# Four graph layers on 32 graphs: new orders on ScalarE and GpSimd at the start, an earlier transposed adjacency matrix, and another order inside layer 1

## The chip, the cores and the metric

The kernel runs on one core of one Trainium2 chip. A core has TensorE (PE, matmuls, with its weight loads listed as PEld), VectorE (DVE), ScalarE (ACT), GpSimd (POOL) and SyncE (SP), whose queue issues all DMAs of this kernel. The metric is the device time of one execution in microseconds. A profile shows one execution; its span runs from the first instruction to the last.

## The reference

`x` holds 32 graphs of 512 nodes with 128 features, `adj` one 512 x 512 matrix for all of them. Four layers follow each other, each adding to x what it makes of `h = max(layernorm(x), 0)`:

```python
# layer 0: attention weights from adj's pattern alone, diagonal and rest with weights of their own
idx = jnp.cumsum(m.reshape(-1).astype(jnp.int32)) - 1          # m = adj > 0
A = jax.nn.softmax(jnp.where(m, e[0][idx].reshape(adj.shape), NEG), axis=1)
out = einsum('ij,bjg->big', A * M, h @ W[0]) + einsum('ij,bjg->big', A * (1 - M), h @ W[1]) + bias
# layer 1: xs = [h, h A, 2 h A A - h, h A, 2 h A A - h] with A = adj (nodes are the contracted axis)
out = jax.nn.relu(concat(xs) @ Theta1 + bias)
# layer 2: weights = adj * adj
messages = jnp.einsum('nm,bnd->bmd', weights, relu(h @ psi_w + psi_b))
out = relu(concat(messages, h) @ phi1_w + phi1_b) @ phi2_w + phi2_b
# layer 3: attention masked by adj
A = jnp.exp(8 * jnp.tanh(Q K^T / sqrt(128) / 8)) * adj;  out = (A / A.sum(-1)) @ h @ v
```

## The kernel before, in words

**Tiles.** Two graphs make a quad, 16 in all; two quads (A and C) make a round, eight rounds, for layers 0 and 1. Layers 2 and 3 go quad by quad. All matmuls that matter are float32.

**Products.** A 512 x 512 matrix times the features of a round is split into 2 x 2 blocks and made with seven block products instead of eight (`products`, L359, in the order `ORDER`, with PSUM banks a, c and d). Their right operands are differences of blocks (`right_steps`, L341, tiles rt_g, rt_h, rt_w, rt_feat, one 128x512 subtraction each, on the engines listed in `engs`); product 6 needs the second of them, and the second is made from the first. Each product's result is taken from its bank by `evict`, mostly on VectorE.

**Beginning (L165 to L680).** By an order written out by hand (`manual_schedule`: all instructions of PE, DVE, ACT and POOL stand as the source has them) the attention matrix of layer 0 is made while the first quads are normalised. Statistics of quads 0 and 1 (`early_stats`) go over POOL, which raises to a power (L211) and multiplies (L212); ScalarE then makes h from x, eight 128x128 tiles a quad (L241). PE turns h (p_hT), ScalarE copies it to hT (L262), and PE projects it (p_g, L428). POOL also makes three parts of e (L556 to L567), which VectorE uses at L607 in `at_part`; `score_rows` (L622, L626) and `softmax_rows` (L633 to L635) make the attention rows. `keep_busy(n)` (L493) issues n matmuls whose result is not used.

**Layer 0 (`round0`, L758).** Also in the order of the source. In the loop over the seven products other work is put in between by hand: `turn(q)` makes hT of quad q (two VectorE transposes into hb at L277, four SP DMAs to the DRAM tile d_hT at L284, one SP DMA back as hT at L286), `projection(q)` makes p_g from hT, `normalise(q)` makes h, `stats` the statistics. `squares` is `turn_adj` (L472): four VectorE transposes of adj (tile adj_squares, L477) and four SP DMAs of 256 KB to adjT_d (L481); layer 3 reads it much later. Before, it stands in round 1: three transposes at product index 1 (L873), the fourth and the DMAs at index 4 (L892). In round 1 p_g of quad 4 comes at index 1, that of quad 5 at index 5; in round 2 p_g of quad 6 comes at index 1.

**Layer 1 (`layer1`, L923).** From here a scheduler places the instructions; generators that take turns (L1133 on) set the order of the source. For a quad, `first` makes x1T = h adj (seven products, p_x1T, evicted by ScalarE and VectorE) and a copy hs; `weighed` projects hs and x1T to w (p_w, 32 matmuls in two banks, copied by ScalarE at L946); then the seven products of adj with w, to whose banks `own` adds projections of hs (p_l, L755). In before a round's steps are: first(A), then first(C) and weighed(A), then weighed(C) and right2 (rt_w, all on POOL), then the products, at the end of them bank e with the fourth own block. Rounds follow each other two steps apart, so PE's order is: products of r, first(C) of r+1, both weighed of r+1, first(A) of r+2, products of r+1.

**Layer 3 (`layer3`).** Scores (p_score), tanh and exponential on ScalarE (L1086, L1088), times adj's transpose (L1090, in turn on VectorE and POOL), then p_av (L1100).

Of the kernel before, what the change touches and what calls it, by code (L numbers as in the profile page):

```python
# [24 lines left out]
def kernel(  # L25
# [106 lines left out]
    def spread(w, n):  # L132
        return w[:, None, :].to_broadcast([P, n, D])

    for b in range(4):
        load_x(b)
    ecol = const.tile([P, NK], F32, name="ecol")
    nc.sync.dma_start(ecol, e_l0.rearrange("o (k p) -> p (o k)", p=P))
    elast = const.tile([P, 1], F32, name="elast")
    nc.sync.dma_start(elast, bass.AP(tensor=e_l0.tensor, offset=e_l0.offset + NE - 1, ap=[[0, P], [1, 1]]))  # L140
    qw = load_rows(q_w, "qw")[:, 0, :]
    kw = load_rows(k_w, "kw")[:, 0, :]
    w0 = const.tile([P, 2, D], F32, name="w0")
# [212 lines left out]

    ORDER0 = (ORDER[0], ORDER[4]) + ORDER[1:4] + ORDER[5:]

    def products(name, form, left, right, evict, order=ORDER):  # L359

        banks = {}
        for k, g, first in order:
            if first:
                banks[g] = bank(f"p_{name}_{g}")
            form(banks[g], left[k], right[k], first)
            evict(k, banks[g])
            yield

# [140 lines left out]
    for t in range(NT):  # L509
        for s in range(t + 1):  # L510
            nc.tensor.matmul(pi[:, t : t + 1], upto[:, s, blk(t)], rch[:, s : s + 1],
                             start=(s == 0), stop=(s == t))
    keep_busy(4)
    early = [early_stats(q, q == 1) for q in range(2)]
    next(early[0])

# [4 lines left out]
    before = prep.tile([P, NT], F32, name="before")  # L521
    nc.vector.tensor_sub(before, incl, rc)
    nc.vector.tensor_scalar(known[:, :, 0], before, float(NE), None, OP.min)
    h = {q: normed_tile(q) for q in range(3)}
    hT = {q: feature_major(f"hT0_{q}") for q in range(4)}
    normal = [normed_steps(q, h[q]) for q in range(3)]
# [24 lines left out]
    nc.scalar.copy(pgs[:, 0:2, :], pg[0])  # L551
    nc.vector.tensor_copy(pgs[:, 2:4, :], pg[1])
    nc.scalar.copy(qkT, tiles(p)[:, :2, :])

    elastn = prep.tile([P, 1], F32, name="elastn")
    nc.gpsimd.tensor_scalar(elastn, elast, -1.0, None, OP.mult)  # L556
    ecoln = prep.tile([P, NK], F32, name="ecoln")
    nc.gpsimd.tensor_scalar(ecoln, ecol, -1.0, None, OP.mult)

    parts = []  # L560
    for i in range(3):
        eh = prep.tile([P, NK], BF16, name=f"eh_{i}")
        nc.gpsimd.tensor_copy(eh, ecoln)
        part = prep.tile([P, NK], F32, name=f"part_{i}")
        nc.gpsimd.tensor_copy(part, eh)
        if i < 2:
            nc.gpsimd.tensor_sub(ecoln, ecoln, part)  # L567
        parts.append(part)
    row_of = prep.tile([P, NK], F32, name="row_of")
    nc.vector.tensor_copy(row_of, pb[:, :, 1])  # L570

# [33 lines left out]
    for kk in range(NK):  # L605
        for i in range(3):
            nc.vector.tensor_scalar(at_part[:, i, kk, :], cols, col_of[:, kk : kk + 1],  # L607
                                    parts[i][:, kk : kk + 1], OP.is_equal, OP.mult)
    go(normal[1], 3)
    go(turned[0])  # L610
    next(project[0])
    go(normal[1])
# [145 lines left out]
    def round0(r):  # L758
# [52 lines left out]
        for i, _ in enumerate(products(f"l0_{r}", by_token, sums["att"], now, evict,  # L811
                                          ORDER if r else ORDER0)):
            if r == 0:
                if i == 0:
                    transpose_rows(pt, att, 2)
                    transpose_rows(pt, att, 3)
                    att_copies((0, 1, nc.scalar.copy), (1, 1, nc.vector.tensor_copy))
                    next(left_of_att)
                    next(left_of_att)
                    go(early_stats_2)  # L820
                    att_copies((2, 1, nc.scalar.copy), (3, 1, nc.scalar.copy))
                elif i == 1:
                    for t in range(NT):
                        nc.tensor.matmul(p_adiag[:, blk(t)], ones, diag[:, t, :], start=True, stop=True)
                    nc.scalar.copy(adiag[0], p_adiag)
                    go(normal[2], NT + 1)
                    diagonal_of(0, 0)
                    go(ln3, NT + 1)
                    go(normal[2])
                    next(left_of_att)  # L830
                    next(left_of_att)
                    go(ln3)
                elif i == 2:
                    diagonal_of(0, 1)
                    add(1, 0, 0)
                elif i == 3:
                    next(turned[2])
                    go(turned[2])
                    add(0, 1, 1)
                    bias(0)  # L840
                    normalise(3)
                    go(ahead[4], NT)
                elif i == 4:
                    upper(held["a"])
                    turned.append(pe_steps(h[3], "hT0_3", hT[3]))
                    next(turned[3])
                    go(ahead[4])
                    add(1, 1, 2)
                    go(projection(2))
                    go(turned[3])  # L850
                    normalise(4)
                    go(ahead[5], NT)
                    bias(1)
                    go(turn(4))
                    go(ahead[5])
                elif i == 5:
                    go(projection(3))
                    go(right_of(1))
                    diagonal_of(1, 0)
                    normalise(5)  # L860
                elif i == 6:
                    go(stats_c, NT)
                continue
            if i == 0:
                if C + 2 < NQ:
                    go(turn(C + 2))
                if A + 4 < NQ:
                    normalise(A + 4)
                diagonal_of(r, 1)
                add(1, 0, 0)  # L870
            elif i == 1:
                add(0, 1, 1)
                if r == 1:  # L873
                    go(squares, 3)
                if more:
                    go(projection(A + 2))
                go(stats_a, NT + 1)
                go(own_a, NT)
                if more:
                    bias(r + 1)  # L880
                go(stats_a)
                go(own_a)
            elif i == 3:
                add(1, 1, 2)
                if not more:
                    next(next_layer)
                if C + 4 < NQ:
                    normalise(C + 4)
                if r >= 3:
                    go(sums_ahead, 2)  # L890
            elif i == 4:
                if r == 1:  # L892
                    go(squares, 3)
                if A + 4 < NQ:
                    go(turn(A + 4))
            elif i == 5:
                if more:
                    go(projection(C + 2))
                    go(right_of(r + 1))
                    diagonal_of(r + 1, 0)  # L900
                go(stats_c, NT + 1)
                go(own_c, NT)
            elif i == 6:
                go(stats_c)
# [18 lines left out]
    def layer1(r):  # L923
# [29 lines left out]
        first(A)  # L953
        turned(C)
        yield
        first(C)
        w1 = quad_tile(f"w_{r}").rearrange("p w e -> p (w e)")[:, : 4 * N]
        w1 = w1.rearrange("p (t b w f) -> p t b w f", t=NT, b=2, w=2)
        weighed(A)
        yield  # L960
        weighed(C)
        right2 = right_blocks(lambda J, b: w1[:, 2 * J : 2 * J + 2, b], f"w_{r}", [nc.gpsimd] * 4)
        yield
        u = [u_tile(f"l1_{r}_{i}") for i in range(3)]
        held = {}

# [2 lines left out]

        def each(y):  # L970
            return y.rearrange("p w (i f) -> p w i f", i=2)

        def spread_bias():
            return b1[:, None, None, :].to_broadcast([P, 2, 2, D])

        def finish(y, I, b):
            x = x_block(r, I, b).rearrange("p w i f -> p w (i f)")
# [6 lines left out]
        def evict(k, p):  # L984
            pv = of_pairs(halves(p))
            if k == 1:
                nc.vector.tensor_add(each(u[0]), pv, spread_bias())
            elif k == 6:
                nc.vector.tensor_add(each(u[1]), pv, each(u[0]))
            elif k == 5:  # L990
                held["d"] = pv
            elif k == 7:
                nc.vector.tensor_add(each(u[2]), pv, each(u[0]))
                nc.vector.tensor_add(each(u[2]), held["d"], each(u[2]))
            elif k == 2:
                own(p, 0, 0, False)
                y = work.tile([P, 2, H], F32, tag="rt", name=f"y1_{r}", bufs=6)
                nc.vector.tensor_add(each(y), pv, spread_bias())
                finish(y, 0, 0)
            elif k == 4:  # L1000
                own(p, 1, 0, False)
                done(p, u[0], 1, 0)
            elif k == 3:
                own(p, 0, 1, False)
                done(p, u[1], 0, 1)

        for _ in products(f"l1_{r}", by_token, sums["adj"], right2, evict):
            pass
        p = bank(f"p_l1_{r}_e")
        own(p, 1, 1, True)  # L1010
        done(p, u[2], 1, 1)
        yield
        if C == NQ - 1:
            yield
            yield
        ln_stats(A)
# [47 lines left out]
    def layer3(q):  # L1064
# [5 lines left out]
        for b in range(2):  # L1070
# [15 lines left out]
                nc.scalar.activation(ex[:, t, :], ps, AF.Tanh, scale=1.0 / (8.0 * math.sqrt(D)))  # L1086
            for t in range(NT):
                nc.scalar.activation(ex[:, t, :], ex[:, t, :], AF.Exp, scale=8.0)  # L1088
                eng = nc.gpsimd if t % 2 else nc.vector
                eng.tensor_mul(split(ex[:, t, :]), split(ex[:, t, :]), crossed(adjTx[0][:, t, :]))  # L1090
            yield
            out_r = out[2 * q + b].rearrange("(t p) f -> p t f", p=P)
# [86 lines left out]
```

## Time and profile before

| | |
|---|---|
| three timed runs | 981.59, 982.46, 981.39 us; median 981.59 |
| the profiled execution | 980.04 us, its span 977.9 us |
| granted TensorE clock, mean | 0.995 |
| matmuls, by stage | beginning to 35.5 us, layer 0 to 196.6, layer 1 to 489.7 (layer 2's first ones mixed in before that), layer 2 to about 692, layer 3 to the end |

A line of the time-ordered list gives the start and duration in microseconds, engine, source line, operation, what is written and read, sizes, and how many instructions were merged; in brackets stands how long the engine had been idle and what ended that. A line of the stage table gives a stretch of time, the busy microseconds and instructions of PE, PEld, DVE, ACT and POOL, then the granted TensorE clock, the busy share of the DMA engines and their GB/s. A line of the list of waits gives who waited for whom, in total, how often, and the longest.

### The profile page before, as it was taken

The page shows a single profiled execution, that of the slowest core. Times are in us where ns is not written, and L with a number is a line of the kernel's source. Part 1 is how long each engine was busy: PE and PEld are TensorE (multiplying, and loading weights), DVE is VectorE, ACT ScalarE, POOL GpSimd, SP SyncE. Part 2 cuts the span into 40 slices and gives each one's busy share as a digit, 9 for nine tenths or more (in the row PEclk, how much of TensorE's full clock was granted, in tenths as well). Part 3 has the DMA queues.
Part 4 walks back from the last instruction along what each step waited for, and adds up shares of the span by engine and source line. Part 5 has one row for each costly group of instructions (what it writes and reads, how often), then busy time and mean ns, then how long its engine had stood idle before and what let it go on. Part 6 is the DMA issues. An engine that isn't in the chain of part 4 may idle for free.

```text
span 977.9 us, 15160 instructions
## 1 busy us (share of the span) xinstructions
PE 959.3 (98%) x5470; PEld 782.7 (80%) x5470; DVE 578.5 (59%) x1322; ACT 471.5 (48%) x1055; POOL 430.1 (44%) x473
## 2 busy tenths in 40 slices
PE   7998999999999999999999999999999999999998
PEld 4788999988988988989977777777667776777776
DVE  6776887656356446557568666556654544444444
ACT  4773453442332232376728544545574455444553
POOL 4676798844437532430624433344132332223322
PEclk8999999999999999999999999999999999999999
DMA  9046554162231311444333333322132121121111
GB/s 256 9 130 173 151 151 114 43 169 65 95 121 44 87 44 44 109 106 110 87 108 99 98 86 85 87 79 73 55 86 77 44 76 54 54 76 44 54 33 44
DMA packets 83914, 86.04 MB, mean 88 GB/s; under 512 B 6785, under 2 KB 74625, under 8 KB 83841
## 3 DMA queue, kind: packets, MB, share of 16 engines
q1 hardware_dynamic: 83840, 85.09, 30.9%
q8 instruction: 43, 0.70, 0.3%
q14 instruction: 31, 0.25, 0.1%
HBM read 44.17 MB, written 40.89 MB: 87 GB/s over the span
## 4 chain that ended last, share of the span: by engine, by line
PE 89%; DVE 4%; ACT 3%; DMA 2%; POOL 1%; issue 1%; SPq 0%; DVEq 0%; ACTq 0%; POOLq 0%
PE p_av L1100 12%; PE p_score L1085 11%; PE p_l_c L379 8%; PE p_l_a L379 5%; PE p_l_d L379 5%; PE p_w L428 5%; PE p_msgT_c L372 4%; PE p_x1T_c L372 4%; PE p_feat L428 3%; PE p_hv L428 3%; PE p_g L428 3%; PE p_msgT_d L372 3%; PE p_msgT_a L372 3%; PE p_qkh L1072 3%; PE p_l L428 3%; PE p_phi L1055 3%
## 5 line engine op out<-in xcount | busy, mean ns | idle before, releaser
L241 ACT ACTIVATE h<-x,sh,rs 128x128 f32<-128x128 f32 x512 | 209.2, 484 | 61.2 <-DVE sh L230 24.6
L1090 POOL TENSOR_TENSOR ex<-ex,adjTx 128x512 f32<-128x512 f32 x64 | 83.2, 1302 | 206.3 <-ACT ex L1088 206.3
L1086 ACT ACTIVATE ex<-p_score 128x512 f32<-128x512 f32 x128 | 71.8, 587 | 124.6 <-issue 113.0
L1100 PEld LDWEIGHTS p_av<-qkh_hv,ex 128*128 128x128 f32 x1024 | 118.5, 191 | 9.4 <-issue 7.4
L1100 PE MATMUL p_av<-qkh_hv,ex 128*128 128x129 f32 x1024 | 120.1, 275 | 0.8 <-POOL ex L1090 0.8
L1085 PE MATMUL p_score<-qkh_hv,hT 128*128 128x512 f32 x256 | 115.2, 593 | 0.0
L277 DVE STREAM_TRANSPOSE hb_hT<-h 128x512 f32<-128x512 f32 x120 | 81.9, 697 | 35.7 <-ACT h L241 35.3
L1090 DVE TENSOR_TENSOR ex<-ex,adjTx 128x512 f32<-128x512 f32 x64 | 45.4, 710 | 82.1 <-ACT ex L1088 82.0
L221 DVE BATCH_NORM_STATS2 bn<-x 128x6 f32<-128x256 f32 x248 | 89.7, 416 | 0.9
L1085 PEld LDWEIGHTS p_score<-qkh_hv,hT 128*128 128x128 f32 x256 | 46.2, 190 | 46.5 <-issue 44.7
L1088 ACT ACTIVATE ex<-ex 128x512 f32<-128x512 f32 x128 | 76.6, 630 | 1.8
L350 POOL TENSOR_TENSOR rt_feat<-feat,feat 128x256 f32<-128x256 f32 x16 | 11.6, 725 | 137.3 <-ACT feat L1039 137.3
L350 POOL TENSOR_TENSOR rt_w<-w 128x512 f32<-128x512 f32 x16 | 20.3, 1268 | 81.2 <-ACT w L946 81.2
L428 PE MATMUL p_w<-th,x1T 128*128 128x128 f32 x256 | 49.5, 275 | 0.0
L428 PE MATMUL p_w<-th,hs 128*128 128x128 f32 x256 | 49.5, 275 | 0.0
L393 ACT COPY x1T<-p_x1T_a 128x256 f32<-128x256 f32 x16 | 5.9, 370 | 84.3 <-PE p_x1T_a L372 84.3
L428 PEld LDWEIGHTS p_hv<-vw,hT 128*128 128x128 f32 x256 | 33.6, 192 | 15.3 <-issue 8.1
L1050 POOL TENSOR_TENSOR x<-x,phi2b 128x256 f32<-128x256 f32 x64 | 44.4, 724 | 0.0
L428 PE MATMUL p_g<-w,hT 128*128 128x128 f32 x256 | 34.9, 295 | 7.9 <-DMA hT<-d_hT 4.3
L1057 ACT ACTIVATE msgT<-p_phi,phi1b 128x512 f32<-128x512 f32 x32 | 21.7, 678 | 40.7 <-PE p_phi L1056 40.7
L428 PEld LDWEIGHTS p_g<-w,hT 128*128 128x128 f32 x256 | 33.4, 209 | 9.6 <-ACT hT L262 4.3
L1105 DVE SCALAR_TENSOR_TENSOR x<-p_av,rsum,x 128x128 f32<-128x128 f32 x128 | 39.1, 347 | 1.9
(231 smaller groups left out, 2066.8 us busy)
## 6 DMA issues: line engine op xcount, KB each, us to landing
d_hT<-hb_hT SPq DMA_DIRECT2D x240, 128.0 KB
hT<-d_hT SPq DMA_DIRECT2D x60, 512.0 KB
x<-in_x_dram SPq DMA_DIRECT2D x32, 256.0 KB
out_dram<-x SPq DMA_DIRECT2D x31, 256.0 KB
adj_s<-in_adj_dram SPq DMA_DIRECT2D x4, 256.0 KB
adjT_d<-adj_squares SPq DMA_DIRECT2D x4, 256.0 KB
sq<-in_adj_dram SPq DMA_DIRECT2D x4, 256.0 KB
adjTx<-adjT_d SPq DMA_DIRECT2D x4, 256.0 KB
```

Source lines behind the costliest of these rows:

```text
L221: nc.vector.bn_stats(st[:, k].rearrange("p e s -> p (e s)"), xt[q][:, b, t : t + 2, :].rearrange("p t f -> p f t"))
L241: nc.scalar.activation(h[:, b, t, :], xt[q][:, b, t, :], AF.Relu, bias=shift[q][:, i : i + 1], scale=scale[q][:, i : i + 1])
L277: nc.vector.transpose(hb[:, :, b].rearrange("p j t r -> p t j r"), h[:, b].rearrange("p t (j c) -> p t j c", c=QR))
L372: nc.tensor.matmul(p[:, :H], b[:, k, :], a[:, k, :], start=(first and k == 0), stop=(k == 1), skip_group_check=True)
L379: nc.tensor.matmul(p[:, i * 2 * D : (i + 1) * 2 * D], a[:, k, blk(i)], b[:, k], start=(first and i == 0 and k == 0), stop=(k == 1), skip_g ...
L428: nc.tensor.matmul(p[:, blk(t)], hT(t), w, start=(i == 0), stop=(i == len(terms) - 1))
L1050: tc.keep_in_program_order(nc.gpsimd.tensor_add(xi, xi, spread(phi2b, 2)))
L1085: nc.tensor.matmul(ps, hT[:, t, b, :], qkh, start=True, stop=True)
L1086: nc.scalar.activation(ex[:, t, :], ps, AF.Tanh, scale=1.0 / (8.0 * math.sqrt(D)))
L1088: nc.scalar.activation(ex[:, t, :], ex[:, t, :], AF.Exp, scale=8.0)
L1090: eng.tensor_mul(split(ex[:, t, :]), split(ex[:, t, :]), crossed(adjTx[0][:, t, :]))
L1100: nc.tensor.matmul(po[:, i, : D + 1], ex[:, t, blk(i0 + i)], hv[:, t, :], start=(t == 0), stop=(t == NT - 1))
```

## The change

At the beginning, two of the first four x loads are issued behind the loads of e; three more `keep_busy` matmuls; POOL's work on e stands ahead of `next(early[0])`, thus ahead of the second half of quad 0's statistics; the three h1 tiles ahead of the copies of hT0 on ScalarE are gone from there (they follow with the other five). In layer 0 `squares` moves from round 1 to round 0, indices 3 and 4; there hT of quad 3 is copied ahead of the projection of quad 2; in round 1 the projection of quad 4 moves from index 1 to index 2.

In layer 1 the steps become: first(A), then weighed(A) and first(C), then nothing (in round 0 weighed(C) and the operands), then weighed(C), the operands and the products. The first operand block is made on VectorE, the other three on POOL. Own blocks b (which takes product 2 too) and e are made directly behind product 1, and e is evicted at product 2. The statistics follow without a step between. PE's order becomes: products of r, weighed(A) and first(C) of r+1, first(A) of r+2, whose last matmuls the scheduler mixes with weighed(C) of r+1, products of r+1. In layer 3, quad 0's first graph has all four products with adj's transpose on VectorE.

```diff
-    for b in range(4):
+    for b in range(2):
         load_x(b)
...
     nc.sync.dma_start(elast, bass.AP(tensor=e_l0.tensor, offset=e_l0.offset + NE - 1, ap=[[0, P], [1, 1]]))
+    for b in range(2, 4):
+        load_x(b)
...
-    keep_busy(4)
+    keep_busy(7)
...
     nc.vector.tensor_scalar(known[:, :, 0], before, float(NE), None, OP.min)
+    elastn = prep.tile([P, 1], F32, name="elastn")
+    nc.gpsimd.tensor_scalar(elastn, elast, -1.0, None, OP.mult)
...
     nc.scalar.copy(qkT, tiles(p)[:, :2, :])
-    elastn = prep.tile([P, 1], F32, name="elastn")
-    nc.gpsimd.tensor_scalar(elastn, elast, -1.0, None, OP.mult)
...
-    go(normal[1], 3)
     go(turned[0])
     next(project[0])
     go(normal[1])
...
                     go(ahead[4], NT)
+                    go(squares, 2)
                 elif i == 4:
...
                     go(ahead[4])
+                    go(squares)
                     add(1, 1, 2)
+                    go(turned[3])
                     go(projection(2))
-                    go(turned[3])
                     normalise(4)
...
-                if r == 1:
-                    go(squares, 3)
-                if more:
+                if more and r > 1:
                     go(projection(A + 2))
...
+            elif i == 2:
+                if r == 1:
+                    go(projection(A + 2))
...
-                if r == 1:
-                    go(squares, 3)
...
-        first(C)
...
         weighed(A)
-        yield
-        weighed(C)
-        right2 = right_blocks(lambda J, b: w1[:, 2 * J : 2 * J + 2, b], f"w_{r}", [nc.gpsimd] * 4)
-        yield
+        first(C)
+        yield
+        def operands():
+            weighed(C)
+            return right_blocks(lambda J, b: w1[:, 2 * J : 2 * J + 2, b], f"w_{r}",
+                                [nc.vector] + [nc.gpsimd] * 3)
+        if r == 0:
+            right2 = operands()
+        yield
+        if r > 0:
+            right2 = operands()
...
             if k == 1:
+                for I, name in ((0, "b"), (1, "e")):
+                    held[name] = bank(f"p_l1_{r}_{name}")
+                    own(held[name], I, I, True)
...
             elif k == 2:
-                own(p, 0, 0, False)
-                nc.vector.tensor_add(each(y), pv, spread_bias())
+                nc.vector.tensor_add(each(y), of_pairs(halves(held["b"])), each(u[0]))
                 finish(y, 0, 0)
+                done(held["e"], u[2], 1, 1)
...
-        p = bank(f"p_l1_{r}_e")
-        own(p, 1, 1, True)
-        done(p, u[2], 1, 1)
-        yield
         if C == NQ - 1:
+            yield
...
-                eng = nc.gpsimd if t % 2 else nc.vector
+                eng = nc.gpsimd if t % 2 and q + b > 0 else nc.vector
```

## The prediction, as it was put on record before the changed kernel ran

> **What bounds the kernel now.** I read the page's engine table first, then who PE waited for, then the time-ordered list around each of those waits.
>
> ```profile
> PE 959.3 (98%) x5470; PEld 782.7 (80%) x5470; DVE 578.5 (59%) x1322; ACT 471.5 (48%) x1055; POOL 430.1 (44%) x473
> ```
>
> TensorE (PE) has matmuls in 98% of the span, and the change removes none: the built program has the same matmuls plus three fillers. So only PE's idle time can be won, 977.9 - 959.3 = 18.6 us, and matmuls that ran slowly. All waits of PE, longest in total first (us, times, longest):
>
> ```profile
> PE p_g L428 <- DMA hT<-d_hT: 4.3, 2, 2.8
> PE p_g L428 <- ACT hT L262: 3.5, 1, 3.5
> PE p_x1T_c L372 <- DVE x1T L395: 2.3, 6, 0.4
> ...
> PE p_av L1100 <- POOL ex L1090: 0.8, 2, 0.6
> PE p_msgT_c L372 <- DVE msgT L395: 0.6, 1, 0.6
> ```
>
> Each of these has a part of the change aimed at it. PE at the two large ones (start, duration):
>
> ```profile
> 14.89 1.53 PE L259 MATMUL p_hT<-ident,h 128*128 128x128 f32 x8
> 19.95 3.78 PE L428 MATMUL p_g<-w,hT 128*128 128x128 f32 x16 [3.54 <-ACT hT L262]
> ...
> 81.91 1.89 PE L379 MATMUL p_l_c<-rt_g,sums_att 128*128 128x256 f32 x8
> 86.56 3.65 PE L428 MATMUL p_g<-w,hT 128*128 128x128 f32 x16 [2.76 <-DMA hT<-d_hT]
> ```
>
> The same 16 projections take 2.05 us at 64.30, but 3.78 and 3.65 after these gaps. The stage table says why (PEclk is the third number from the right):
>
> ```profile
> 20.00:25.00 5.00, 5.00 (x20) 4.07 (x21) 0.37 (x1) 2.32 (x6) 0.00 (x0) 0.50 1.02 247
> ...
> 87.00:90.00 3.00, 3.00 (x16) 3.00 (x15) 0.67 (x3) 0.58 (x1) 3.00 (x4) 0.50 1.07 318
> ```
>
> After a gap of about 3 us the granted clock is 0.50 for some microseconds; after the 1.50 us gap at 62.80 it stayed 1.00.
>
> [...] the 512-byte packets of adjT_d started from 74.5 to 80.6, and the 1 KB packets of the d_hT behind them nearly all after 79.5.
>
> **Part A, the beginning.** What holds p_g until 19.95 is ScalarE's order (L609 puts three tiles of h1 ahead of the copies of hT0):
>
> ```profile
> 14.39 1.65 ACT L241 ACTIVATE h<-x,sh,rs 128x128 f32<-128x128 f32 x4
> 18.17 1.26 ACT L241 ACTIVATE h<-x,sh,rs 128x128 f32<-128x128 f32 x3 [2.14 <-POOL sh L212]
> 19.34 1.04 ACT L262 COPY hT<-p_hT 128x512 f32<-128x512 f32 x2
> ```
>
> The h1 tiles wait for POOL's sh. Afterwards the copies follow h0 directly: 16.05 to 17.05, the second after the transposes (16.42). p_g started 0.09 after the first copy's end, so it starts at 16.6 instead of 19.95. No gap, so full clock: 16 x 0.112 = 1.8, done at 18.4. score_rows(0) then needs at_part, which DVE still finishes at 19.04 (unchanged): p_val(0) ends at about 20.3 instead of 26.27.
>
> From there ScalarE limits. POOL's eleven small operations on e (13.64 to 16.11) move ahead of its wait for the second half of quad 0, into its idle 9.37 to 12.39 (3.02 us); they need 2.5. Their loads are issued 1.1 us earlier, behind two x tiles instead of four; two x tiles are issued 1.9 us later, and DVE reads those only at 13.02. So rs of quad 1 follows DVE's sh at 14.75, h1 can start at 16.85, runs 17.05 to 20.3, and exp(0) starts when least(0) is there, 21.1 instead of 27.05. From exp(0) to the first p_l_a took 8.46; walked through in the new order I get 8.7, so p_l_a starts at 29.8 instead of 35.51: **5.7 us** (4.5 if ScalarE's queue is tighter than I count, 6.0 at best). The three fillers cost 3 x 0.216 = 0.65 inside the 0.98 us that PE waits before 9.33: nothing.
>
> **Part B, adj's squares in round 0.** Before, four DVE transposes (0.63 to 0.70 each) and four SP DMAs (issued 73.87 to 77.24) stood ahead of d_hT of quad 6, and p_g(6) waited until 86.56. Gone from there, quad 6's chain is: transposes at 73.2 to 74.5; 3.7 us from first d_hT issue to hT's issue (as at 98.25 to 101.96) and 3.5 to landing (60.80 to 64.26): 81.7. PE comes at 83.7. The gap of 2.76 and the slow clock (3.65 - 1.79) vanish: **4.6 us** (2.8 if a wait remains).
>
> Round 0 now pays. DVE gets two transposes at 46.3 (it idles 0.93 at 46.3, so u2 is 0.35 late; POOL uses it at 50.49) and two after sh of quad 4, 51.8 to 53.1; the statistics behind them end at 54.5, where quad 4's own transposes stood before. ScalarE copies hT3 first (L850 ahead of L849) and so reaches h4 at 51.8 instead of 52.89: quad 4's DMAs are issued at 56.0 instead of 56.98. But adjT_d, issued from 53.15, is ahead of them in the ring. Before, adjT_d's first issue to d_hT's landing took 82.95 - 73.87 = 9.1, so d_hT(4) lands at 62.3, not 60.7, and hT(4) at 65.8. p_g(4) now stands one product (1.73) later, at 62.80 + 1.73 = 64.5. It waits 1.3 instead of 1.5; hT(5) gets 1 us later and just meets its use. **0.1 us** (-0.9 to +0.8). Times here are on the clock of before.
>
> **Part C, layer 1.** Before, each round's last products p_l_d and p_l_e are followed at once by x1T, whose second p_x1T_c waits for a DVE that is still finishing x and its statistics:
>
> ```profile
> 238.88 1.03 PE L372 MATMUL p_x1T_c<-sums_adj,rt_h 128*128 128x256 f32 x4
> 239.75 1.03 PE L372 MATMUL p_x1T_d<-sums_adj,rt_h 128*128 128x256 f32 x4
> 241.19 1.10 PE L372 MATMUL p_x1T_c<-adj_s,rt_h 128*128 128x256 f32 x4 [0.42 <-DVE x1T L395]
> ```
>
> Starts are 0.87 apart, here 1.44: 0.57 lost. Eight such places (0.37, five of 0.58, 0.15, 0.23) make 3.65. After, 32 projections (3.57 us) of weighed(A) stand between, and the e block is evicted early, so DVE has some 3 us of work and over 5 us for it: no wait.
>
> The new risk is on the other side: weighed(C) now directly precedes its products. From the end E of the last x1T_d, whose h buffer ScalarE waits for (+0.28, as at 209.45): four h tiles 1.63, copy of w 0.56, three h tiles 1.22, second copy 0.57: E + 4.27. DVE's rt_w_0, priced at 0.69 (a 128x512 float32 product of L1090 took that), and POOL's rt_w_1, 1.27, with 0.08 per hand-over: E + 6.5. PE meanwhile has 28 more projections (3.12), p_l_a 1.73, b and e 0.89 each: E + 6.63. It fits by 0.14. Behind rt_w_0 on DVE wait one hb transpose and u0; behind rt_w_1 on POOL the other two blocks, used 3.5 us and more later. On ScalarE the two roots for the statistics (L227) now stand between the two copies of the next round's w, which is first used some 12 us later. I take **3.0** of the 3.65 (0.5 if each of the seven rounds after the first lacks 0.45; 3.7). POOL loses eight blocks of 1.27; DVE's 59% takes them.
>
> **Parts D and E.** After the last round of layer 1, p_msgT_c lost 0.8 in the same way: **0.4** (0 to 1.0, the order there is reshuffled). In layer 3's first block POOL's two products end at 701.75. Four on DVE at 0.69, each after its exponential (the last at 699.75), end at 701.0: **0.7** (0.4 to 1.1); the statistics behind them are 1.5 later, and ScalarE idles 2.0 there before its next scores.
>
> **Sum:** 5.7 + 0.1 + 4.6 + 3.0 + 0.4 + 0.7 = 14.5 us of this profile's 977.9 us span. The timed runs (981.4 to 982.5) and this one's 980.0 are within 0.3% of each other; I subtract from the median: 981.6 - 14.5 = 967.1.
>
> **Rivals.**
> - Layer 1's new chain is longer than counted and takes part C back (3.0 becomes -0.5): 970.6. For it: 0.14 us of room. Against: all its durations are from rows. Chance 0.14.
> - Round 1's wait for hT(4) grows beyond some 2 us behind adjT_d, and the clock halves as it did at 87: 0.9 more wait, 1.9 slow, 970.0. Against: 1.5 did not do it. Chance 0.10.
> - ScalarE or a late load takes half of part A: 969.9. Chance 0.10.
> - Slower: DVE's rt_w_0 is queued behind an hb transpose that waits for an hb buffer, which is free only when an earlier quad's d_hT DMAs have landed. If those land late, rt_w_0, POOL and p_l_c are late in each of the seven later rounds. To undo 11.5 us from the other parts and be 2 us slower, it must cost 13.5 / 7 = 1.9 per round, so it decides once that transpose ends 2.1 us after the copy of w. Then 983.6. Against: in before the DMAs of 249.42 have landed at 253.45, and a quad comes every 17 us. Chance 0.04.
> - The edits do nothing, because PE is bound elsewhere: 981.6, chance 0.02. The listed waits speak against it.
>
> The forecast has the remaining 0.60. Low end: all best values, 6.0 + 0.8 + 4.6 + 3.7 + 1.0 + 1.1 = 17.2, 964.4. High end: the worst of each, 4.5 - 0.9 + 2.8 + 0.5 + 0 + 0.4 = 7.3, 974.3, which covers the first three rivals. A measurement of this kernel can tell about 0.2%, 2 us, from no change: faster 0.94, same 0.02, slower 0.04.
>
> **What would show it.** A: p_g at about 16.6 and PEclk 1.00 between 18 and 25, p_l_a near 29.8. B: no clock of 0.50 in the first 100 us, p_g(6) without wait, p_g(4) still waiting about 1.3. C: p_x1T_c without waits, p_l_c with at most 0.1 for rt_w. E: no POOL wait of p_av. I am wrong if PE's idle time falls by much less than 12 us, if p_l_c waits for POOL in layer 1, or if a new 0.50 stretch appears.

## The result and the profile after

The changed kernel took 970.98 us (median of four, 970.44 to 971.69), the kernel before 981.49 us beside it: ratio 0.9894, interval 0.9877 to 0.9911. So 10.5 us less, where 14.5 were forecast. The forecast was made from one profile, and runs of the kernel before differ with the mean clock they were granted: of the 39 beside the experiments, those at 0.998 took 977.2 to 978.3 us, those at 0.994 or 0.995 took 979.4 to 981.6.

The page's engine table and the list of PE's waits, after (columns as before):

```profile
PE 956.6 (99%) x5473; PEld 780.9 (81%) x5473; DVE 584.6 (60%) x1332; ACT 471.1 (49%) x1055; POOL 421.1 (43%) x463
...
PE p_g L431 <- DMA hT<-d_hT: 2.1, 2, 1.2
...
PE p_msgT_a L375 <- ACT feat L1051: 0.9, 1, 0.9
PE p_msgT_c L375 <- POOL rt_feat L352: 0.7, 1, 0.7
PE p_l_a L382 <- ACT w L949: 0.7, 1, 0.7
PE p_msgT_c L375 <- DVE msgT L398: 0.6, 1, 0.6
PE p_msgT_a L375 <- ACT msgT L396: 0.5, 1, 0.5
...
PE p_x1T_c L375 <- DVE x1T L398: 0.2, 1, 0.2
```

The waits of p_g for ScalarE and of p_av for POOL are gone, and of the six of p_x1T_c one is left. But p_g still waits twice for hT, and, besides one wait at the first loads, four rows are new: p_msgT_a twice, p_msgT_c for POOL, p_l_a. PE's time-ordered list and the stage table at the places shown before:

```profile
16.07 1.53 PE L261 MATMUL p_hT<-ident,h 128*128 128x128 f32 x8
17.74 2.05 PE L431 MATMUL p_g<-w,hT 128*128 128x128 f32 x16
...
60.93 2.02 PE L431 MATMUL p_g<-w,hT 128*128 128x128 f32 x16 [1.16 <-DMA hT<-d_hT]
...
70.87 2.05 PE L431 MATMUL p_g<-w,hT 128*128 128x128 f32 x16 [0.96 <-DMA hT<-d_hT]
...
79.73 1.95 PE L431 MATMUL p_g<-w,hT 128*128 128x128 f32 x16
```

```profile
20.00:25.00 5.00, 5.00 (x26) 2.39 (x24) 3.76 (x9) 3.97 (x11) 0.00 (x0) 1.00 1.00 255
...
87.00:90.00 3.00, 3.00 (x22) 2.79 (x22) 2.31 (x4) 1.09 (x3) 1.57 (x2) 1.00 0.35 141
```

The first 16 p_g (2.05 us) and those of quad 6 (1.95) run without a wait, at a granted clock of 1.00. Those of quads 4 and 5 wait: one old wait, one new.

To see where the time came from, I cut every profile at five starts on PE: p_incl (the first matmuls that need adj), the first p_l_a, the first p_x1T, the first p_phi, the first p_score. All values in us, each the difference of two such starts, the last one to the span's end:

| kernel | to p_incl | beginning | layer 0 | layer 1 | layer 2 | layer 3 | span |
|---|---|---|---|---|---|---|---|
| before | 7.08 | 28.43 | 161.13 | 293.04 | 202.90 | 285.36 | 977.9 |
| after | 8.27 | 22.48 | 157.35 | 294.43 | 202.93 | 284.33 | 969.8 |
| begin_act | 7.87 | 22.48 | 159.05 | 293.04 | 202.92 | 285.36 | 970.7 |
| begin_fill | 7.95 | 25.89 | 163.64 | 293.06 | 202.98 | 285.37 | 978.9 |
| after_old_loads | 7.91 | 22.25 | 157.34 | 294.47 | 202.98 | 284.33 | 969.3 |
| layer1_only | 8.55 | 27.39 | 159.63 | 294.43 | 202.98 | 285.36 | 978.3 |
| after_last_now | 7.88 | 22.49 | 157.40 | 291.29 | 202.95 | 284.61 | 966.6 |
| after_squares_behind | 8.21 | 22.48 | 157.23 | 294.45 | 202.94 | 284.33 | 969.6 |
| after_rtw_pool | 7.18 | 22.50 | 157.35 | 296.20 | 202.98 | 284.33 | 970.5 |
| both | 8.03 | 22.43 | 159.20 | 291.30 | 202.96 | 284.62 | 968.5 |
| after_squares_last | 7.43 | 22.47 | 154.73 | 294.72 | 202.97 | 284.34 | 966.7 |
| both_last | 8.22 | 22.45 | 154.73 | 291.56 | 202.92 | 284.62 | 964.5 |

From before to after: beginning -5.95, layer 0 -3.78, layer 1 +1.39, layer 3 -1.03, together 9.4; the wait for the first loads was 1.19 longer in this profile, so its span shows 8.1. **Layer 1, priced at a gain of 3.0 (part C), lost 1.4.** This is where it lost, PE's list at the end of layer 1 after:

```profile
449.68 1.03 PE L375 MATMUL p_x1T_d<-sums_adj,h 128*128 128x256 f32 x4
450.54 1.95 PE L431 MATMUL p_feat<-psi,hT 128*128 128x128 f32 x16
453.39 1.13 PE L375 MATMUL p_msgT_a<-sq,feat 128*128 128x256 f32 x4 [0.91 <-ACT feat L1051]
455.04 0.70 PE L375 MATMUL p_msgT_a<-sq,feat 128*128 128x256 f32 x2 [0.52 <-ACT msgT L396]
456.46 1.13 PE L375 MATMUL p_msgT_c<-sums_sq,rt_feat 128*128 128x256 f32 x4 [0.72 <-POOL rt_feat L352]
```

In the last round there is no first(A) of a round two ahead. Weighed(C) has moved to one step later, and in its old place stand the first products of layer 2, made from a feat that came out of PE just before. PE waits for each link of their chain.

### The profile page after: what moved, and what is told of

It is laid out like the page before. It is cut to its first block, busy times and chain, and to the rows that moved or that the text cites. A ratio compares the mean times of both kernels' runs of the same rounds, so it can differ in the third digit from the quotient of the medians.

```text
span 969.8 us, 15164 instructions
## 1 busy us (share of the span) xinstructions
PE 956.6 (99%) x5473; PEld 780.9 (81%) x5473; DVE 584.6 (60%) x1332; ACT 471.1 (49%) x1055; POOL 421.1 (43%) x463
## 4 chain that ended last, share of the span: by engine, by line
PE 90%; DVE 3%; POOL 2%; ACT 2%; DMA 1%; issue 1%; SPq 0%; DVEq 0%; POOLq 0%; ACTq 0%
PE p_av L1112 12%; PE p_score L1097 11%; PE p_l_c L382 7%; PE p_w L431 5%; PE p_l_d L382 5%; PE p_msgT_c L375 5%; PE p_x1T_c L375 4%; PE p_l_a L382 4%; PE p_hv L431 3%; PE p_l L431 3%; PE p_qkh L1084 3%; PE p_msgT_d L375 3%; PE p_feat L431 3%; PE p_phi L1067 3%; PE p_phi L1068 3%; PE p_msgT_a L375 3%
## 5 line engine op out<-in xcount | busy, mean ns | idle before, releaser
L1102 POOL TENSOR_TENSOR ex<-ex,adjTx 128x512 f32<-128x512 f32 x62 | 80.4, 1297 | 208.2 <-ACT ex L1100 202.6
L949 ACT COPY w<-p_w 128x512 f32<-128x512 f32 x32 | 18.2, 574 | 106.2 <-PE p_w L431 106.1
L352 POOL TENSOR_TENSOR rt_w<-w,rt_w 128x512 f32<-128x512 f32 x16 | 20.3, 1270 | 110.3 <-DVE rt_w L352 92.0
L431 PEld LDWEIGHTS p_w<-th,hs 128*128 128x128 f32 x256 | 39.9, 192 | 0.7
L1051 ACT ACTIVATE feat<-feat 128x512 f32<-128x512 f32 x32 | 20.1, 629 | 40.9 <-DVE feat L1050 40.9
L700 POOL TENSOR_TENSOR hd<-hT,adiag 128x512 f32<-128x512 f32 x32 | 39.7, 1276 | 0.3 <-ACT adiag L827 0.3
```

Source lines behind the costliest of these rows:

```text
L431: nc.tensor.matmul(p[:, blk(t)], hT(t), w, start=(i == 0), stop=(i == len(terms) - 1))
```

## The experiments

All ratios are to the kernel before, run beside. The changed kernel was not timed again beside these runs, so differences to it are read from the stretches of the table. "Excess" is how much later a matmul starts than its predecessor's usual duration allows.

**One line of the beginning (begin_act).** On the kernel before:

```diff
-    go(normal[1], 3)
```

> The kernel before with one line less: the three h1 tiles no longer stand ahead of the two copies of hT0 on ScalarE. Theory (ScalarE's order alone held p_g): p_g starts at about 16.6 instead of 19.95, PEclk stays 1.00 between 18 and 25, the first p_l_a comes at about 30.5 instead of 35.51, so 5 us less (976.5). Rival (the loads of e and POOL's order are needed too): p_g starts early but exp(0) stays late, p_l_a comes after 33, 2.3 us less or nothing.

973.68 us, ratio 0.9933 (0.9918 to 0.9949). PE's list and ScalarE's, begin_act:

```profile
17.33 2.05 PE L428 MATMUL p_g<-w,hT 128*128 128x128 f32 x16
...
30.34 1.99 PE L379 MATMUL p_l_a<-g,attT 128*128 128x256 f32 x8
```

```profile
15.16 1.65 ACT L241 ACTIVATE h<-x,sh,rs 128x128 f32<-128x128 f32 x4
16.71 1.10 ACT L262 COPY hT<-p_hT 128x512 f32<-128x512 f32 x2
18.94 0.49 ACT L241 ACTIVATE h<-x,sh,rs 128x128 f32<-128x128 f32 x1 [1.13 <-POOL sh L212]
```

The beginning is 22.48, exactly that of the changed kernel. ScalarE does wait for POOL's sh before h1 here, and loses almost nothing by it: exp(0) follows the eighth h1 tile at 22.03, and least(0), which it needs too, comes at 21.9. So in these profiles the removed line is the whole of part A; POOL's order, the loads' and the fillers add nothing to it. The time fell by more than the beginning's 5.95, since layer 0 is 2.08 shorter too: p_g of quad 6 waited 2.47 here (2.76 before), and the granted clock stayed 1.00 after it: its 16 matmuls took 2.02 (3.65 before).

**Fillers in the gaps (begin_fill).** On the kernel before, ahead of the p_g of quads 0 and 6, into the bank that p_g then starts anew:

```diff
+        if name == "p_g_0_0":
+            for _ in range(15):
+                nc.tensor.matmul(p, upto[:, 0, blk(0)], upto[:, 0, :], start=True, stop=True)
+        if name == "p_g_6_0":
+            for _ in range(6):
+                nc.tensor.matmul(p, w0[:, 1, :], adj_s[:, 0, :], start=True, stop=True)
```

> The kernel before with matmuls whose result is not used in PE's two long gaps: 15 of 0.22 us ahead of the p_g that waits until 19.95, 6 of 0.43 us ahead of the one that waits until 86.56. The waits themselves stay. Theory (PE's idle time lowers the granted clock): PEclk stays 1.00 after both, the 16 p_g take about 2.05 and 1.8 instead of 3.78 and 3.65, 2 to 4 us less (979.5 to 977.5). Rival (the clock falls for another reason, such as the burst that follows): p_g takes 3.7 as before and the time stays 981.5.

979.13 us, ratio 0.9994 (0.9984 to 1.0004): no difference that can be told in the time, but two readings in the profile. PE's list and the stage table, begin_fill:

```profile
17.12 3.40 PE L428 MATMUL p_g<-upto 128*128 128x512 f16 x15
20.82 2.05 PE L434 MATMUL p_g<-w,hT 128*128 128x128 f32 x16 [0.30 <-ACT hT L262]
...
62.99 3.38 PE L434 MATMUL p_g<-w,hT 128*128 128x128 f32 x15 [1.87 <-DMA hT<-d_hT]
```

```profile
20.00:25.00 5.00, 4.65 (x29) 2.98 (x29) 1.07 (x2) 3.18 (x8) 0.00 (x0) 1.00 1.12 274
...
64.00:67.00 3.00, 3.00 (x16) 2.95 (x15) 3.00 (x9) 0.98 (x3) 3.00 (x4) 0.56 1.08 327
```

With the first gap filled the clock from 20 to 25 is 1.00 (0.50 before), p_g takes 2.05 (3.78 before), and the beginning is 2.54 shorter than before (1.50 shorter than in layer1_only, which has the same gap and a mean clock of 0.66 from 20 to 25), though p_g still waits for hT, until 20.82: here the idle gap, not the burst after it, lowered the clock. But the gap of 1.87 before p_g of quad 4 was followed by a clock of 0.56 from 64 to 67 (the view ends behind 15 of the 16 matmuls, at 3.38). The profiled execution, 980.98 us, is one of four of the twelve near 981; the other eight took 978.6 to 979.2 at a mean clock of 0.999 or 1.000, too high for 3.4 us at 0.50, which would take 0.002 off the mean. The second filler was mis-sized: its 6 float32 matmuls appear in the trace as 12 instructions and took 5.1 us (83.95 to the p_g at 89.10) instead of 2.6, and p_g of quad 6 started 6.87 after the p_l_c ahead of it, instead of 4.65. This filler tells nothing.

**The loads in the old order (after_old_loads).** On the changed kernel:

```diff
-    for b in range(2):
+    for b in range(4):
         load_x(b)
...
-    for b in range(2, 4):
-        load_x(b)
```

> The changed kernel with the loads in the old order (four x tiles, then e). Theory (the small packets of e, issued two x tiles earlier, hold up the last tiles of adj): the third tile of adj is used at 4.95 instead of 6.59, p_incl starts at 7.1 instead of 8.27, the first p_l_a at 29.6 instead of 30.75, so 1.2 us less than the changed kernel (969.8). Rival (the landing of the first loads varies from run to run whatever their order): p_incl anywhere from 7.1 to 8.3, and no difference to 971.0.

973.0 us (970.59 to 975.81), ratio 0.9927 (0.9899 to 0.9954): no gain. Two of the four runs took 974.8 and 975.8 at a mean clock of 0.998; the profile is of another, 971.2, so where those two lost 4 us stays open. p_incl came at 7.91; among kernels with the loads of before it ranged from 7.08 to 8.55, with the new order from 7.18 to 8.27. The theory is not borne out: the landing of the first loads varies by over 1 us by itself, and two spans can be compared only from p_incl on.

**The new layer 1 alone (layer1_only).** The kernel before with the layer 1 of the change (the diff above, from `first(C)` to the `yield` of `C == NQ - 1`).

> The kernel before with the new layer 1 alone. Theory (the new step removes the waits of p_x1T_c but leaves the first messages of layer 2 without other products beside them): the waits of p_x1T_c fall from 3.65 to about 0.4, p_msgT_a and p_msgT_c of quad 0 wait 2.2 to 2.7, one p_l_a may wait 0.8: together 1.3 us more than before (982.8). Rival (the waits around 452 come from the other parts, which shift ScalarE's work against PE's): no wait at the first messages, 2 to 3 us less (979).

980.74 us, ratio 1.0010 (1.0000 to 1.0020). Layer 1 is 294.43 as in the changed kernel, and the waits for feat, msgT and rt_feat are the same 0.9, 0.5 and 0.7. Layer 1's loss is made by its own edit, whatever stands before it. PE's list of layer1_only also shows a long gap after which the clock did not fall (1.00 from 83 to 87, and from 87 to 90):

```profile
87.12 2.02 PE L429 MATMUL p_g<-w,hT 128*128 128x128 f32 x16 [3.05 <-DMA hT<-d_hT]
```

**The last round as the first (after_last_now).** On the changed kernel:

```diff
-        if r == 0:
+        if r == 0 or C == NQ - 1:
             right2 = operands()
         yield
-        if r > 0:
+        if 0 < r and C < NQ - 1:
             right2 = operands()
```

> The changed kernel, but in the last round of layer 1 the weighed projections of C and the operands come one step earlier, as in its first round. Theory (in the last round nothing of layer 1 is left to stand beside the first products of layer 2): the 32 p_w matmuls stand between p_x1T and the first p_msgT, the three waits at 452 to 456 (2.64 us by starts) go, 2.0 to 2.7 us less than the changed kernel (968.3 to 969). Rival (layer 2's first quad is held by ScalarE's h tiles and waits just as long later): PE's waits for feat and rt_feat stay over 2 us, no difference.

968.25 us, ratio 0.9881 (0.9865 to 0.9898). PE's list, after_last_now:

```profile
450.21 1.95 PE L431 MATMUL p_feat<-psi,hT 128*128 128x128 f32 x16
452.00 0.39 PE L431 MATMUL p_w<-th,hs 128*128 128x128 f32 x2
...
455.35 0.39 PE L431 MATMUL p_w<-th,x1T 128*128 128x128 f32 x2
455.57 1.03 PE L375 MATMUL p_msgT_a<-sq,feat 128*128 128x256 f32 x4
456.44 1.03 PE L375 MATMUL p_msgT_c<-sums_sq,rt_feat 128*128 128x256 f32 x4
```

The 32 p_w stand between p_feat and its user, and no wait is left. Layer 1 falls from 294.43 to 291.29, 3.14 less: the excess of the messages' starts at this place was 1.07 + 0.68 + 0.89 = 2.64, and the rest are hand-overs of about 0.1 behind each wait (the four p_msgT_a take 1.13 in after, 1.03 here). Shown: the moved step itself is a gain of 1.75 (293.04 - 291.29), and its last round cost 3.14. Of these, 0.28 are lost again in layer 3 (284.61 against 284.33), here and in the two later runs with this edit.

**All operands on POOL (after_rtw_pool).** On the changed kernel:

```diff
-                                [nc.vector] + [nc.gpsimd] * 3)
+                                [nc.gpsimd] * 4)
```

> The changed kernel with all four operand blocks of layer 1 on POOL, as before the change. Theory of the prediction (the chain from the copy of w through rt_w to p_l_c has 0.14 us of room): 0.58 us more for the first block makes p_l_c wait about 0.45 us in each of seven rounds, 3 us more than the changed kernel (974). Rival (the chain has more room than counted): no wait of p_l_c, 971.0.

972.39 us, ratio 0.9926 (0.9912 to 0.9939). Layer 1 is 1.77 longer; p_l_c starts late for POOL in six rounds, 0.29 each on average (0.23 to 0.49). The result lies between the two: in the changed kernel rt_w_1 ends about 0.5 before p_l_c starts (251.96 and 252.44, for one), more room than the 0.14 counted, and less than POOL's extra time. The first block on VectorE is needed.

**The squares behind quad 6 (after_squares_behind).** On the changed kernel, `squares` out of round 0, and in round 1:

```diff
                 add(0, 1, 1)
+                if r == 1:
+                    go(squares, 3)
...
                     go(turn(A + 4))
+                if r == 1:
+                    go(squares)
```

> The changed kernel with adj's squares back in round 1 (three transposes at index 1), but the fourth and the DMAs to adjT_d behind the whole turn of quad 6, not ahead of it. p_g of quad 4 stays at index 2. Theory (the four DMAs of 256 KB ahead of d_hT of quad 4 in the queue make p_g of quads 4 and 5 wait): both waits go (1.33 and 1.12 us by starts), that of quad 6 stays away, 2.4 us less than the changed kernel (968.6). Rival (d_hT of quad 4 is late for other reasons, such as DVE and ScalarE work before it): p_g(4) waits over 1 us as before; or p_g(6) or p_g(7) waits instead, no difference or a loss.

971.89 us, ratio 0.9925 (0.9907 to 0.9942): no gain. Quads 4 to 6 wait no more, but PE's list of after_squares_behind shows a wait at quad 7, the first whose d_hT is issued behind adjT_d, and a bank late on VectorE:

```profile
86.13 1.99 PE L382 MATMUL p_l_c<-rt_g,attT 128*128 128x256 f32 x8 [0.55 <-DVE u_l L789]
...
89.95 2.02 PE L431 MATMUL p_g<-w,hT 128*128 128x128 f32 x16 [0.94 <-DMA hT<-d_hT]
```

Layer 0 is 157.23 against 157.35. The rival holds: in each of the three places tried (here, before and in the changed kernel) a p_g waits for the d_hT that comes behind adjT_d (0.94, 2.76 and 1.16).

**That and the last round (both).** Both edits on the changed kernel.

> The changed kernel with both edits: the last round's weighed projections a step earlier, and the squares' DMAs behind the turn of quad 6. If both waits are causes of their own: 2.64 + 2.45 = 5 us less than the changed kernel (966). If one of them only moves the wait: 968 to 971.

969.73 us, ratio 0.9898 (0.9882 to 0.9913). Layer 1 again gains its 3.1, but here p_g of quad 7 waited 2.10 and ran its 16 matmuls in 3.42 (the clock from 91 to 94 was 0.53), so layer 0 was 159.20.

**The squares where nothing is turned (after_squares_last).** On the changed kernel, `squares` out of round 0, and:

```diff
-        ab = last.tile([P, N // QR, NT, QR], F32, tag="x", name="adj_squares")
+        ab = quad_tile("adj_squares").rearrange("p w e -> p (w e)")[:, : NT * N]
+        ab = ab.rearrange("p (j t c) -> p j t c", t=NT, c=QR)
...
                 add(1, 0, 0)
+                if r == 7:
+                    go(squares, 2)
             elif i == 1:
                 add(0, 1, 1)
+                if r == 7:
+                    go(squares)
```

> The changed kernel with adj's squares in round 7 (indices 0 and 1), where no quad of layer 0 is turned any more; their tile takes a buffer that a g of an earlier round has left. p_g of quad 4 stays at index 2. Theory (adj's squares with their DMAs cost PE what d_hT behind them waits, wherever in rounds 0 to 2 they stand): without them no p_g waits for hT, the stretch from the first p_l_a to the first p_x1T shrinks from 157.35 to about 154.9, 2.4 us less than the changed kernel (968.5). Rival (the squares' DVE work or DMAs hold up layer 1's first x1T instead): new waits of p_x1T or p_w between 185 and 210 take most of it back, 970 to 971.

968.95 us, ratio 0.9886 (0.9871 to 0.9900). No p_g waits for hT any more, and layer 0 is 154.73, 2.62 less. One wait of p_x1T_c grew by 0.26 (excess 0.36 to 0.62, at 187.85), part of layer 1's 0.29 more. What moved away is VectorE work as well as DMAs, and the traces tell them apart. In the changed kernel quad 4's transposes into hb end at 51.11, no later than here (50.26, in a run whose p_incl is 0.84 earlier); but from its first d_hT issue to that of hT it takes 5.60 (51.85 to 57.45), here 3.82 (50.42 to 54.24). So it is the queue. Quad 5 inherits it: in SP's order its d_hT (59.96) stands behind hT of quad 4 and four x loads. PE's list of after_squares_last, quad 4:

```profile
57.03 1.89 PE L382 MATMUL p_l_d<-rt_g,sums_att 128*128 128x256 f32 x8
58.75 1.95 PE L431 MATMUL p_g<-w,hT 128*128 128x128 f32 x16
```

**Both at their best (both_last).** after_squares_last and after_last_now together.

> The changed kernel with the squares in round 7 and, in the last round of layer 1, the weighed projections of C a step earlier. The first edit is measured beside it, the second took 3.14 us from layer 1's stretch; if they add up, 2.4 + 3.1 = 5.5 us less than the changed kernel (965.5). If round 7's squares disturb layer 1: 967 to 968.

966.24 us (965.92 to 966.38), ratio 0.9857 (0.9840 to 0.9873): faster than both kernels. The two add up, 2.62 and 2.87 less in layers 0 and 1 than after, with 0.29 more in layer 3. PE's longest waits that remain, of both_last:

```profile
PE p_idle L497 <- DVE upto L186: 1.9, 1, 1.9
PE p_l_a L382 <- ACT w L952: 0.7, 1, 0.7
PE p_msgT_c L375 <- DVE msgT L398: 0.6, 1, 0.6
```

## Why the prediction was right, and where it was not

The measured 970.98 lies in the range given, and the changed kernel is faster; the likeliest value, 967.1, was 3.9 us too low. That the sum held is in part the luck of a wide range (gains of 7.3 to 17.2): one part had the wrong sign, and one of the prediction's own signs of being wrong came true, PE's idle time fell by 5.4 us (18.6 to 969.8 - 956.6 = 13.2) and not by about 12.

- **Part A, 5.7: right, 5.95.** From p_incl, which the first loads set, p_g was forecast at 16.6 - 7.08 = 9.5 and came at 9.47; p_l_a at 22.7 and came at 22.48. But of its four edits one does it all, and the walk through POOL and the loads priced things that PE does not wait for. (The operations on e are ten, not eleven, and took 2.9, not 2.5: 10.50 to 13.42.) The size is also that of one profile: layer1_only, with the same gap, needed 27.39 for the beginning, 1.04 less than before.
- **Part B, round 2, 4.6: right, 4.62** between the two profiles. It is the price of this one profile of before, though: 2.9 of it is the gap, and 1.7 the slow clock after it, which begin_act and layer1_only had not after gaps of 2.5 and 3.1 at the same place (2.02 for the 16 p_g in both).
- **Part B, round 1, 0.1: mis-sized, -0.85.** The old wait for hT of quad 4 stayed as forecast (1.33 by starts, 1.67 before), but hT of quad 5, said to just meet its use, was 1.12 late. The queue behind adjT_d was followed for one quad, and for the next only as 1 us.
- **Part C, 3.0: wrong, and the step that failed.** "Rounds follow each other two steps apart" was taken for all eight rounds. The walk was right for the inner ones: no p_l_c waits, five waits of p_x1T_c are gone. Inside, 1.75 came of the forecast 3.0, since one p_l_a waits 0.84 for a copy of w that stands behind eight h tiles on ScalarE, and the interleaved p_w and p_x1T cost some small hand-overs. The last round, which has no first(A) behind it, was not walked, and cost 3.14.
- **Part D, 0.4: nothing.** p_msgT_c still starts 0.78 late at 515.43 (0.77 at 522.58 before); VectorE's statistics stand before its eviction as they did.
- **Part E, 0.7: right, 1.03** in layer 3's stretch (0.75 in the three runs with the last round's edit).
- **The rivals.** The time fell on that of the first (970.6), but not by its mechanism: no p_l_c waits for rt_w, and after_rtw_pool shows the room. The slower case, rt_w_0 held up by an hb transpose, is not seen in any of eight rounds. Nor are the other two: the clock stayed 1.00 after round 1's waits of 1.16 and 0.96 (the "some 2 us" of that rival was an estimate between the gaps of 1.50 and 2.76 of before), and part A came whole.

Part D lies in layer 2's stretch, which did not change (202.90 and 202.93). The sum by stretches is 5.95 + 3.78 - 1.39 + 1.03 = 9.4, inside the interval of the timed difference (0.9 to 1.2%, 8.7 to 12.1 us).

## What to carry to other kernels

Walk a changed software pipeline through its first and its last round too, where the step that hid a chain has nothing left to put beside it; here the last round took 3.14, more than the 1.75 that the moved step gave in all. Of an edit in several parts, try the smallest alone: here one removed line was the whole of the beginning. A bulk transfer that nobody needs soon belongs where no transfer that PE soon waits for follows it in the queue: here it took 5.60 from quad 4's first d_hT issue to that of hT behind adjT_d, and 3.82 without. Moved among such transfers it only changes whose wait it is.

## What was not expected of the hardware

How long PE idled did not alone decide whether its clock fell. The gaps ahead of p_g, by length, with the mean granted clock of a stretch behind each and the time that the 16 p_g took:

| kernel | p_g starts at | gap | stretch | granted clock in it | the 16 p_g |
|---|---|---|---|---|---|
| before | 64.30 | 1.50 | 64 to 67 | 1.00 | 2.05 |
| begin_fill | 62.99 | 1.87 | 64 to 67 | 0.56 | 15 of them 3.38 |
| both | 90.05 | 2.10 | 91 to 94 | 0.53 | 3.42 |
| begin_act | 80.95 | 2.47 | 82 to 85 | 1.00 | 2.02 |
| before | 86.56 | 2.76 | 87 to 90 | 0.50 | 3.65 |
| layer1_only | 87.12 | 3.05 | 87 to 90 | 1.00 | 2.02 |
| layer1_only | 21.4 | 3.5 | 20 to 25 | 0.66 | - |
| before | 19.95 | 3.54 | 20 to 25 | 0.50 | 3.78 |

Nor was the fall equally long each time: in the profile of before the clock was 0.50 from 18.42 to 25.25, where it fell while PE still waited, and from 86.69 to 90.10. With the gap of 3.54 filled it stayed 1.00 (begin_fill), so that gap was needed for its fall. What decided among the gaps of 1.87 to 3.05 was not shown: no run moved a gap by itself and left its length.

And the same first loads landed over 1 us earlier or later from run to run: in the kernels with the loads of before, p_incl came from 7.08 to 8.55.
